# A four-layer network on one core: the group norm's deviation moved to ScalarE, its small products paused, and one step of layer 0 reordered

## The chip, the cores and the metric

The kernel runs as one program on one core of a Trainium2 chip. The metric is the device time of one execution in microseconds (us), the median over several runs. The core has five instruction queues: TensorE (PE: matrix products and transposes), VectorE (DVE), ScalarE (ACT), GpSimd (POOL) and SyncE (SP, which here issues the DMAs). Each queue runs its instructions in its own order, and semaphores join them.

## The reference, cut to what matters

The input `x` is 16 images of 192 channels and 32 × 32 positions, float32. Four residual layers follow one another, each on the group norm of what came before:

```python
# GN: 32 groups of 6 channels, eps 1e-5, no learned scale or shift
def group_norm(x):                       # x: (16, 192, 32, 32)
    g = x.reshape(16, 32, -1)
    g = (g - g.mean(-1, keepdims=True)) / sqrt(g.var(-1, keepdims=True) + 1e-5)
    return g.reshape(x.shape)

x = x + layer0(group_norm(x))   # mLSTM block (12 heads of 32) + SiLU(linear) branch, 3x3 conv, batch norm, leaky relu
x = x + layer1(group_norm(x))   # Mamba block: state-space scan with 16 states
x = x + layer2(group_norm(x))   # depthwise conv, batch norm, relu6
x = x + layer3(group_norm(x))   # scan in 4 directions (SS2D) + local conv branch, mixed by a softmax router
```

This is a sketch of the structure in short names; the batch norms of layers 0 and 2 use statistics over all 16 images, so each of them ends a stage of the program. A group norm is wanted once per image and layer: 64 times.

## The kernel before, in words

Channels lie on partitions (192 as 2 × 96), positions along the free axis. The mean of a group of 6 channels crosses partitions, so `group_norm` works in four stages. DVE takes each channel's mean and variance (`bn_stats`, L351, and `bn_aggr`, L352). A 96 × 96 product on PE with a constant matrix gives the groups' means (L355, 2 columns). DVE forms each channel's deviation from it and its square plus the variance (L357 to L362). A second such product gives the groups' variances (L365). DVE then adds eps (L367) and POOL raises to the power -0.5 (L309, in `pow_mhalf`), which gives the tile `gnr`. The caller scales the image on DVE: `layer0_image` (L543), `layer1_front` (L1240), `layer1_tail` (for layer 2, L1351) and `layer3_front` (L1545).

Layer 0 runs over 128 chunks of 128 positions, 8 for an image. Four chunks make a unit of 512 positions. The loop `for g in range(n + 2)` drives `layer0_step`, which yields up to 8 times for a chunk, and after each yield `side.tick(g + j / 8)` may run a piece of the side tasks. The steps are:

1. `down`, the projection of a unit finished two chunks before;
2. four DVE products `p` of scores and decays (L753), the POOL product `vr` (L755), at a unit's first chunk the unit's decays on PE (`layer0_decays`, L686 and L689), and the next chunk's row of exponents by DMA (`layer0_row`, L700, tile `e`);
3. the carried state times the queries (L767), the weighted values `num` (L779), and two POOL sums on `e` (L705 the mask, L706);
4. the new state (L806) and the exponential of `e` on ACT (L711);
5. the next chunk's scores (L722, first part of `layer0_scores`);
6. transposes of its keys `k` (to `kt`, copied by DVE, L728) and of its values (L733; to `v`, copied by ACT, L736), the second part of `layer0_scores`;
7. the former chunk's output transposes (`layer0_output`, L851), their product with a gate on DVE (`ht`, L854) and a sum on POOL (L857);
8. the norm of the heads (`layer0_norm`, L828 to L841, with Ln and Exp on ACT in L839 and L840).

The side tasks have a window each, from a start to an end in chunks, and are run by it: `image` loads an image and normalises it; `front` does a unit's layer norm (L377 and L385 on PE), up projection (L569, its copies on ACT L571 and L573), convolution, SiLU (L596), query and key projections (L607, key copy L613) and gates, and ends with L619 on ACT, L622 on POOL and three L625 on ACT; `spread` writes a finished image to memory and reads it back as `ya` and `yb`; three `conv` tasks apply the 3 × 3 convolution (L520).

The order on PE is set in two ways. The main instructions of a step are tied to one another in program order by `Chain`:

```python
def __call__(self, ins):
    if self.last is not None:
        self.tc.add_manual_dep(ins.ins, self.last, why)   # NoSync: an order, not a wait
    self.last = ins.ins.name
    return ins
```

The side tasks' products are not tied; a scheduler places them, and everything on the other engines, by its own costs. PE's results for side tasks and for most small steps go to PSUM tiles called `mm`, of which two rotate; a third such product waits until the first one's reader is done.

Layers 1 to 3 share a scan (`scan_run`): for each unit of 512 positions and each of 16 states, in three thirds, ACT makes decays `da` (L986, five buffers) and scaled inputs `xbt` (L966), PE transposes them (`xb`, L994 and L997, three buffers), DVE scans (L1010), POOL multiplies by `c` (L1017) and PE transposes back and sums (`y`, L1028). PE's order there is tied by a list of its own, `in_order`. Loads, group norms and projections of the next images are again side tasks.

Of the kernel before, what the change touches and what calls it, by code (L numbers as in the profile page):

```python
# [19 lines left out]
HP = 96  # L20
# [223 lines left out]
class Chain:  # L244
# [5 lines left out]
    def __call__(self, ins):  # L250
        if self.last is not None:
            why = mybir.DependencyInfo(mybir.DependencyClass.NoSync, mybir.DependencyReason.DATA)
            self.tc.add_manual_dep(ins.ins, self.last, why)
        self.last = ins.ins.name
        return ins
# [19 lines left out]
class Program:  # L275
    def __init__(self, tc, ins, out, at):
        self.tc, self.nc, self.ins, self.out = tc, tc.nc, ins, out
        self.at96, self.at128, self.atc, self.atc0 = at
        self.nb = ins["x"].shape[0]

# [63 lines left out]
    def group_norm(self, pool, psum, x):  # L344

        nc = self.nc
        st = pool.tile([HP, 2, 2, 6], F32, name="gnst")
        mv = pool.tile([HP, 2, 2], F32, name="gnmv")
        for m in range(2):
            for i, h in enumerate(halves()):  # L350
                nc.vector.bn_stats(st[:, m, i], x[:, m, h])  # L351
            nc.vector.bn_aggr(mv[:, m], st[:, m].rearrange("p a b -> p (a b)"))  # L352
            yield 1
        ps = psum.tile([128, 512], F32, name="mm")
        nc.tensor.matmul(ps[:HP, :2], self.k("group", HP), mv[:, :, 0], start=True, stop=True)  # L355
        mean = pool.tile([HP, 2], F32, name="gnmean")
        nc.vector.tensor_copy(mean, ps[:HP, :2])  # L357
        d = pool.tile([HP, 2], F32, name="gnd")
        nc.vector.tensor_tensor(d, mv[:, :, 0], mean, SUB)
        q = pool.tile([HP, 2], F32, name="gnq")  # L360
        nc.vector.tensor_tensor(q, d, d, MUL)
        nc.vector.tensor_tensor(q, q, mv[:, :, 1], ADD)  # L362
        yield 1
        ps = psum.tile([128, 512], F32, name="mm")
        nc.tensor.matmul(ps[:HP, :2], self.k("group", HP), q, start=True, stop=True)  # L365
        r = pool.tile([HP, 2], F32, name="gnr")
        nc.vector.tensor_scalar(r, ps[:HP, :2], EPS, None, ADD)  # L367
        self.pow_mhalf(r)
        yield 1
        return mean, r, d  # L370
# [22 lines left out]
    def layer0(self):  # L393
        tc = self.tc
        with (
# [13 lines left out]
            self.main = Chain(tc)  # L409
            for b in range(1, self.nb):  # L410
                side.add("image", self.layer0_image(b, sp, bp, psum), 8 * b - 5.1, 8 * b - 4)
            for i in range(1, self.nb * S // U):
                side.add("front", self.layer0_front(i, sp, bp, dp, psum), NCH * i - 3.9, NCH * i - 1.2)
            for b in range(self.nb - 1):
                side.add("spread", self.layer0_spread(b, wp, dp), 8 * b + 9, 8 * b + 9.1)
                for j in range(3):
                    at = 8 * b + 9.6 + 2.4 * j
                    side.add("conv", self.layer0_conv2(b, j, bp, psum), at, at + 2.4)
# [11 lines left out]
            side.close()  # L430
            finish(self.layer0_spread(self.nb - 1, wp, dp))
# [307 lines left out]
    def layer0_step(self, g, n, chunks, sp, bp, psum):  # L739
# [52 lines left out]
        if new:  # L792
            yield from self.layer0_scores(new, bp, psum)
        if g - 1 in chunks:
            self.layer0_output(chunks[g - 1], bp, psum)
            yield
        if k:
# [143 lines left out]
    def scan_run(self, units, side, bp, psum):  # L941
# [7 lines left out]
        last = []  # L949

        def in_order(ins):

            if last:
                self.tc.add_manual_dep(
                    ins.ins, last.pop(), mybir.DependencyInfo(mybir.DependencyClass.NoSync, mybir.DependencyReason.DATA)
                )
            last.append(ins.ins.name)
# [97 lines left out]
        for i in range(len(steps) - 2, len(steps)):  # L1055
            for t in range(3):
                total(i, t)
        side.close()
# [11 lines left out]
    def layer12(self):  # L1070
        tc = self.tc
        with (
# [7 lines left out]
            self.rep = 18 * (W + 2), 6  # L1080
            self.stats = wp.tile([HP, 2, 2 * self.nb, 6], F32, name="stats")
# [295 lines left out]
    def layer3(self):  # L1377
        tc = self.tc
        with (
# [7 lines left out]
            self.rep = 19 * (W + 3), 4  # L1387
            self.image = {}
# [322 lines left out]
```

## Time and profile before

| what | us |
|---|---|
| median of 3 runs | 17,355.21 (17,339.39 to 17,372.06) |
| the profiled execution | 17,403.5, its span 17,401.7 |
| PE busy | 15,749.6 (91% of the span) |
| DVE busy | 13,122.0 (75%) |
| ACT busy | 11,873.6 (68%) |
| POOL busy | 11,450.8 (66%) |
| layer 0 | about 0 to 3,860 |
| layers 1 and 2 | about 3,860 to 7,620 |
| layer 3 | about 7,622 to 17,402 |

The profile is of one execution. An engine's busy time says how near it is to being the limit over the whole span; the stages differ, so the waits have to be read in the stage that holds them. In a group of instructions the numbers are the count, the busy time, the mean of one and the idle time ahead of them with what ended it. `PEclk` is the clock that TensorE was granted, in tenths.

### The profile page before, as it was taken

Reading aid. Unit: us, or ns where it says so; the run is one execution under the profiler, and the core shown is the slowest. Engines: PE = TensorE matmul, PEld = TensorE weight load, DVE = VectorE, ACT = ScalarE, POOL = GpSimd, SP = SyncE. Lnnn points to the kernel's source line nnn. Section 1 sums busy time; section 2 is a strip of 40 time slices with the busy share of each in tenths; the row PEclk is TensorE's granted clock in tenths of the full one; section 3 lists DMA queues with packets and bytes.
Section 4 is the critical chain, followed back from the end, with each engine's and each line's share of the span. In section 5 each row is a group of like instructions: output and inputs, shape, how many; then the busy total and the mean of one; then the engine's idle time right before and its main releaser. Section 6 shows DMA issues by size and latency. Waiting matters only on the chain. (4 is left out here: it accounts for less than half of the span.)

```text
span 17401.7 us, 263068 instructions
## 1 busy us (share of the span) xinstructions
PE 15749.6 (91%) x99452; PEld 11013.2 (63%) x99452; DVE 13122.0 (75%) x14859; ACT 11873.6 (68%) x19637; POOL 11450.8 (66%) x5555
## 2 busy tenths in 40 slices
PE   8998988888988899979899999999999999999998
PEld 4444444435555555547777777777777777777777
DVE  4444444437777777749889888888888888888888
ACT  3222322327666666648888888888888888888888
POOL 3333333425555555538788788888878888888888
PEclk8889998989999999989999999999999999999999
DMA  1111111123333343433333333323333333333332
GB/s 51 42 40 44 44 43 44 47 63 107 114 110 110 113 118 116 118 99 103 90 99 107 93 96 101 107 83 99 107 98 92 99 108 88 96 105 102 88 98 67
DMA packets 890141, 1544.65 MB, mean 89 GB/s; under 512 B 83472, under 2 KB 314653, under 8 KB 879530
## 3 DMA queue, kind: packets, MB, share of 16 engines
q1 hardware_dynamic: 888874, 1527.81, 30.3%
q8 instruction: 788, 12.91, 0.3%
q14 instruction: 479, 3.92, 0.1%
HBM read 1284.22 MB, written 243.27 MB: 88 GB/s over the span
## 5 line engine op out<-in xcount | busy, mean ns | idle before, releaser
L1017 POOL TENSOR_TENSOR h<-h,cb 128x1536 f32<-128x1536 f32 x2560 | 8872.8, 3469 | 1432.0 <-DVE h L1010 902.9
L986 ACT ACTIVATE da<-dt,neg_a 128x512 f32<-128x512 f32 x7680 | 5267.0, 714 | 1752.0 <-DVE h L1010 1687.3
L1010 DVE TENSOR_TENSOR_SCAN h<-da,carry,xb 128x512 f32<-128x512 f32 x3840 | 4652.4, 1262 | 657.1 <-PE xb L997 596.2
L1028 PE MATMUL y<-const,h 128*128 128x128 f32 x30720 | 4717.9, 276 | 128.3 <-DVE ysum L1468 54.0
L1010 DVE TENSOR_TENSOR_SCAN h<-da,xb 128x512 f32<-128x512 f32 x3840 | 4440.6, 1202 | 388.7 <-PE xb L997 270.7
L994 PE MATMUL xb<-const,xbt 128*128 128x128 f32 x23040 | 4074.6, 282 | 422.5 <-DVE h L1010 269.3
L966 ACT ACTIVATE xbt<-ut,bt 128x384 f32<-128x384 f32 x7680 | 4174.4, 603 | 246.4 <-PE xb L994 244.3
L994 PEld LDWEIGHTS xb<-const,xbt 128*128 128x128 f32 x23040 | 2757.2, 143 | 1815.5 <-issue 643.8
L1028 PEld LDWEIGHTS y<-const,h 128*128 128x128 f32 x30720 | 3684.9, 143 | 322.8 <-issue 265.4
L997 PE MATMUL xb<-diag,ut 128*128 128x128 f32 x15360 | 3016.4, 279 | 0.0
L997 PEld LDWEIGHTS xb<-diag,ut 128*128 128x128 f32 x15360 | 2383.5, 195 | 63.1 <-issue 63.1
L830 POOL TENSOR_TENSOR hs<-h,mhm 128x384 f32<-128x384 f32 x128 | 108.5, 848 | 1685.1 <-DVE den L835 1290.5
L1016 POOL COPY carry<-h 128x3 f32<-128x3 f32 x1280 | 250.5, 196 | 1220.1 <-DVE h L1010 964.7
L976 POOL TENSOR_TENSOR diag<-const,bt 128x512 f32<-128x512 f32 x640 | 680.8, 1064 | 550.5 <-PE xb L997 362.1
L705 POOL TENSOR_TENSOR e<-e,const 128x1536 f32<-128x1536 f32 x128 | 439.9, 3437 | 288.9 <-DMA e<-row 273.0
L520 PE MATMUL conv<-ya,w_conv 128*64 128x512 f32 (+1 forms) x1152 | 543.9, 656 | 66.1 <-DMA ya<-yrows 62.2
L916 PE MATMUL mm<-dbl,w_dt 45*128 45x512 f32 x960 | 532.8, 639 | 33.6 <-DVE v L1490 16.2
L711 ACT ACTIVATE e<-e 128x1536 f32<-128x1536 f32 x128 | 189.7, 1482 | 417.7 <-POOL e L706 417.4
L854 DVE TENSOR_TENSOR ht<-sz,mm 128x384 f32<-128x384 f32 x128 | 70.7, 552 | 519.5 <-PE mm L851 519.5
L1171 PE MATMUL mm<-rep,t_dw 96*32 96x512 f32 x2304 | 433.5, 614 | 23.5 <-DMA rep<-xr 17.3
L779 PEld LDWEIGHTS num<-v,p 128*128 128x128 f32 x3072 | 389.3, 201 | 102.2 <-issue 77.9
L920 DVE SCALAR_TENSOR_TENSOR dt<-lnsq,mm 128x512 f32<-128x512 f32 x480 | 322.0, 671 | 171.9 <-ACT lnsq L919 171.9
(272 smaller groups left out, 17910.1 us busy)
## 6 DMA issues: line engine op xcount, KB each, us to landing
cb<-row SPq DMA_DIRECT2D x2560, 256.0 KB
rep<-xr SPq DMA_DIRECT2D x384, 331.0 KB
e<-row SPq DMA_DIRECT2D x128, 768.0 KB
rep<-xin SPq DMA_DIRECT2D x384, 256.0 KB
rep<-xr SPq DMA_DIRECT2D x384, 228.8 KB
x<-x SPq DMA_DIRECT2D x48, 768.0 KB
xr<-xin SPq DMA_DIRECT2D x48, 612.5 KB
xr<-xpad SPq DMA_DIRECT2D x32, 867.0 KB
```

The lines of the kernel that those rows point to most:

```text
L520: nc.tensor.matmul(o, self.w_c2[:k, t, c0 : c0 + o.shape[0]], src[:k, r0 : r0 + 16, dx : dx + W], start=t == 0, stop=t == 14, skip_group_c ...
L705: nc.gpsimd.tensor_tensor(k.e, k.e, self.k0("mask")[:, None, :].to_broadcast([128, NH, 128]), ADD)
L916: nc.tensor.matmul(ps, w_dt[:, t * 128 : (t + 1) * 128], dbl, start=True, stop=True)
L966: nc.scalar.activation(t[:, c], u.ut[:, c], AF.Copy, scale=u.bt[:, c, n : n + 1])
L976: nc.gpsimd.tensor_tensor(d, ident[:, None, :].to_broadcast([128, 4, 128]), u.bt[:, 3, n : n + 4][:, :, None].to_broadcast([128, 4, 128]), ...
L986: nc.scalar.activation(da[i, t], u.dt[:, t], AF.Exp, scale=u.neg_a(t, n))
L994: in_order(nc.tensor.transpose(xb[i, t][:, c * 128 : (c + 1) * 128], xbt[i][:, c, t * 128 : (t + 1) * 128], ident))
L997: in_order(nc.tensor.matmul(xb[i, t][:, 384:], u.ut[:, 3, t * 128 : (t + 1) * 128], u.diag[n // 4][:, n % 4], start=True, stop=True, skip_ ...
L1010: nc.vector.tensor_tensor_scan(hv, dv, xv, 0.0 if first else u.carry_in[:, n, t : t + 1], MUL, ADD)
L1017: nc.gpsimd.tensor_tensor(h[i], h[i], u.c.pop(n)[:, None, :].to_broadcast([128, 3, 512]), MUL)
L1028: in_order(nc.tensor.matmul(u.y[:, j], h[i][:, t, c * 128 : (c + 1) * 128], ident, is_transpose=True, start=n == 0 and j % 4 == 0, stop=n ...
L1171: self.nc.tensor.matmul(ps[32 * g : 32 * g + 32], blocks[:, g * side + r], seen, start=r == 0, stop=r == side - 1, skip_group_check=True,)
```

## The change

In `group_norm`, the generator now yields a pause before each of its two small products, so that the side scheduler resumes it no sooner than a set number of steps later: 0.15 chunks in layer 0, 0.7 scan steps in layers 1 and 2, 1.2 in layer 3. Each product is placed behind the last main instruction on PE (`behind`, which orders without becoming part of the chain). The deviation is made by two ACT instructions, Ln with eps as its bias and Exp with scale -0.5, in place of DVE's sum and POOL's power. One `Chain` now serves all layers, and takes the place of `in_order`'s list.

In layer 0 the image task's window moves from 8b - 5.1 ... 8b - 4 to 8b - 6.2 ... 8b - 4.6. The conv tasks start at 8b + 9.9 + 2.3j in place of 8b + 9.6 + 2.4j, with windows of 2.3 in place of 2.4 chunks. In `layer0_step` the former chunk's output transposes stand between the scores and the transposes of `k` and `v`; before they followed both.

The counts change so: 64 DVE instructions (L367) and 64 POOL instructions (L309) fewer, 128 ACT activations more; PE's instructions are the same in number.

```diff
--- before.py
+++ after.py
@@ -247,10 +247,15 @@
     def __init__(self, tc):
         self.tc, self.last = tc, None
 
-    def __call__(self, ins):
+    def behind(self, ins):
+
         if self.last is not None:
             why = mybir.DependencyInfo(mybir.DependencyClass.NoSync, mybir.DependencyReason.DATA)
             self.tc.add_manual_dep(ins.ins, self.last, why)
+        return ins
+
+    def __call__(self, ins):
+        self.behind(ins)
         self.last = ins.ins.name
         return ins
 
@@ -277,6 +282,7 @@
         self.tc, self.nc, self.ins, self.out = tc, tc.nc, ins, out
         self.at96, self.at128, self.atc, self.atc0 = at
         self.nb = ins["x"].shape[0]
+        self.main = Chain(tc)
 
 
     def v96(self, name, i=0, n=1):
@@ -351,8 +357,11 @@
                 nc.vector.bn_stats(st[:, m, i], x[:, m, h])
             nc.vector.bn_aggr(mv[:, m], st[:, m].rearrange("p a b -> p (a b)"))
             yield 1
+        yield Wait(self.pause)
         ps = psum.tile([128, 512], F32, name="mm")
-        nc.tensor.matmul(ps[:HP, :2], self.k("group", HP), mv[:, :, 0], start=True, stop=True)
+        self.main.behind(
+            nc.tensor.matmul(ps[:HP, :2], self.k("group", HP), mv[:, :, 0], start=True, stop=True)
+        )
         mean = pool.tile([HP, 2], F32, name="gnmean")
         nc.vector.tensor_copy(mean, ps[:HP, :2])
         d = pool.tile([HP, 2], F32, name="gnd")
@@ -361,11 +370,12 @@
         nc.vector.tensor_tensor(q, d, d, MUL)
         nc.vector.tensor_tensor(q, q, mv[:, :, 1], ADD)
         yield 1
+        yield Wait(self.pause)
         ps = psum.tile([128, 512], F32, name="mm")
-        nc.tensor.matmul(ps[:HP, :2], self.k("group", HP), q, start=True, stop=True)
+        self.main.behind(nc.tensor.matmul(ps[:HP, :2], self.k("group", HP), q, start=True, stop=True))
         r = pool.tile([HP, 2], F32, name="gnr")
-        nc.vector.tensor_scalar(r, ps[:HP, :2], EPS, None, ADD)
-        self.pow_mhalf(r)
+        nc.scalar.activation(r, ps[:HP, :2], AF.Ln, bias=self.k("eps", HP))
+        nc.scalar.activation(r, r, AF.Exp, scale=-0.5)
         yield 1
         return mean, r, d
 
@@ -406,16 +416,16 @@
             self.unit, self.image = {}, {}
             n = self.nb * S // 128
             side = Side()
-            self.main = Chain(tc)
+            self.pause = 0.15
             for b in range(1, self.nb):
-                side.add("image", self.layer0_image(b, sp, bp, psum), 8 * b - 5.1, 8 * b - 4)
+                side.add("image", self.layer0_image(b, sp, bp, psum), 8 * b - 6.2, 8 * b - 4.6)
             for i in range(1, self.nb * S // U):
                 side.add("front", self.layer0_front(i, sp, bp, dp, psum), NCH * i - 3.9, NCH * i - 1.2)
             for b in range(self.nb - 1):
                 side.add("spread", self.layer0_spread(b, wp, dp), 8 * b + 9, 8 * b + 9.1)
                 for j in range(3):
-                    at = 8 * b + 9.6 + 2.4 * j
-                    side.add("conv", self.layer0_conv2(b, j, bp, psum), at, at + 2.4)
+                    at = 8 * b + 9.9 + 2.3 * j
+                    side.add("conv", self.layer0_conv2(b, j, bp, psum), at, at + 2.3)
             finish(self.layer0_image(0, sp, bp, psum))
             finish(self.layer0_front(0, sp, bp, dp, psum))
             self.layer0_decays(self.unit[0], sp, psum)
@@ -428,6 +438,7 @@
                 for j, _ in enumerate(self.layer0_step(g, n, chunks, sp, bp, psum)):
                     side.tick(g + j / 8)
             side.close()
+            self.main.last = None
             finish(self.layer0_spread(self.nb - 1, wp, dp))
             for j in range(3):
                 finish(self.layer0_conv2(self.nb - 1, j, bp, psum))
@@ -789,11 +800,14 @@
             if new:
                 self.layer0_decay(new)
             yield
-        if new:
-            yield from self.layer0_scores(new, bp, psum)
+        scores = self.layer0_scores(new, bp, psum) if new else iter(())
+        for _ in scores:
+            yield
+            break
         if g - 1 in chunks:
             self.layer0_output(chunks[g - 1], bp, psum)
             yield
+        yield from scores
         if k:
             self.layer0_norm(k, h, sp, bp)
             yield
@@ -946,15 +960,9 @@
         ident = self.k("ident")
         steps = [(u, n) for u in units for n in range(NS)]
         xbt, xb, da, h = {}, {}, {}, {}
-        last = []
-
-        def in_order(ins):
-
-            if last:
-                self.tc.add_manual_dep(
-                    ins.ins, last.pop(), mybir.DependencyInfo(mybir.DependencyClass.NoSync, mybir.DependencyReason.DATA)
-                )
-            last.append(ins.ins.name)
+
+        in_order = self.main
+        in_order.last = None
 
         def times_b(i):
             if i >= len(steps):
@@ -1055,6 +1063,7 @@
         for i in range(len(steps) - 2, len(steps)):
             for t in range(3):
                 total(i, t)
+        in_order.last = None
         side.close()
 
     def untranspose(self, y, t, psum):
@@ -1078,6 +1087,7 @@
         ):
             self.layer1_weights(wp, dp, psum)
             self.rep = 18 * (W + 2), 6
+            self.pause = 0.7
             self.stats = wp.tile([HP, 2, 2 * self.nb, 6], F32, name="stats")
             self.image = {b: {} for b in range(self.nb)}
             side, units = Side(), []
@@ -1385,6 +1395,7 @@
         ):
             self.layer3_weights(wp, bp, dp)
             self.rep = 19 * (W + 3), 4
+            self.pause = 1.2
             self.image = {}
             side, units = Side(), []
             carry = [wp.tile([128, NS, 3], F32, name=f"carry{i}") for i in range(2)]
```

## The prediction

> **What bounds the kernel now.** I read the page's first two parts, then the stretches of the layers, then PE's waits inside layer 0 and who waited for the tile `gnr`. The page first (busy time and share of the span; then tenths busy in 40 slices, and the granted clock in tenths):
>
> ```profile
> PE 15749.6 (91%) x99452; PEld 11013.2 (63%) x99452; DVE 13122.0 (75%) x14859; ACT 11873.6 (68%) x19637; POOL 11450.8 (66%) x5555
> ...
> PE   8998988888988899979899999999999999999998
> ...
> PEclk8889998989999999989999999999999999999999
> ```
>
> PE is the bound throughout; its clock is low only in the first nine slices, layer 0. The stretches are layer 0, layers 1 and 2, and layer 3 (busy us by engine, then clock, DMA share, GB/s):
>
> ```profile
> 0.00:3620.00 3620.00, 3217.96 (x13679) 1630.35 (x13680) 1725.53 (x3452) 1072.12 (x1594) 1369.68 (x846) 0.88 0.18 44
> 3900.00:7600.00 3700.00, 3297.46 (x19328) 2152.27 (x19328) 2759.32 (x3002) 2489.65 (x3973) 2100.95 (x1023) 0.97 0.38 112
> 7622.00:17400.00 9778.00, 9005.87 (x65536) 7120.08 (x65536) 8543.64 (x8204) 8257.47 (x13985) 7913.15 (x3640) 0.97 0.33 97
> ```
>
> In layer 0 PE idles 402 us of 3,620 while the other engines are under half busy: it waits for results late in a queue, not for a full engine. In layer 3 PE, DVE, ACT and POOL are all above 80%. PE's waits in layer 0 (engine, line, what ended the wait: us in all, times, longest):
>
> ```profile
> PE mm L377 <- DVE x L543: 96.8, 15, 7.6
> PE mm L851 <- ACT v L736: 63.1, 22, 4.9
> PE conv L520 <- DMA ya<-yrows: 51.9, 14, 4.9
> PE mm L851 <- DVE kt L728: 43.1, 27, 3.5
> ...
> PE mm L607 <- ACT v L736: 16.0, 15, 1.3
> PE mm L365 <- ACT v L736: 15.2, 13, 1.6
> ```
>
> The six sum to 286 us, 19 us for each of 15 later images. The first is the group norm's own: the unit's projection L377 stands waiting for the normalised image. The tile `gnr` in the whole kernel, first its operations, then its waits:
>
> ```profile
> L367 DVE TENSOR_SCALAR gnr<-mm x64: 122/145/156, 33.5 to 16416.9; 96x2 f32<-96x2 f32 x64
> L309 POOL TENSOR_TENSOR gnr<-gnr,const x64: 679/690/709, 33.7 to 16417.9; 96x2 f32<-96x2 f32 x64
> L543 DVE TENSOR_SCALAR x<-x,gnmean,gnr x32: 798/1394/4699, 34.4 to 3458.7; 96x1024 f32<-96x1024 f32 x32
> ...
>   DVE x L543: 56.3, 16
>   DVE xpad L1545: 24.5, 16
>   DVE xf L1240: 10.9, 16
> ...
>   DVE xpad L1351: 3.2, 4
> ```
>
> The last four rows are DVE waiting for POOL's power: 94.9 us, 52 times. One more wait matters, ACT's in layer 0:
>
> ```profile
> ACT sz L625 <- POOL xact L622: 191.3, 30, 8.2
> ```
>
> **What the Trainium skill says.** "Perfetto Trace Analysis", in "Tensor Engine Instruction (MATMUL, LD_WEIGHTS)", states that ACT, DVE and GpSimd are strict FIFOs: an instruction that waits holds all behind it. The row for L625 agrees: ACT stands 6.4 us a time in front of it. "TensorE: Matmul & The Clock Gate", Part 1, "What's actually happening": the clock halves after an idle window of about 3.4 us and returns after a busy one. The clock of 0.88 in layer 0 against 0.97 agrees; its dips to 0.50 last about 3.4 us or a multiple, and mostly follow idle stretches near 4 us. "ScalarE: Activation LUTs", "Table sets": exp and ln share one table set. The trace has such a pair (L839 212 ns, L840 205 ns), with 2.1 us of idle in all before 121 L840s, so no load lies between them. "SBUF — State Buffer", "SBUF: two separate sides": DVE and GpSimd lock a shared port against each other. L543's 0.80 to 4.70 us for one shape fits.
>
> **The change, part by part.**
>
> *The deviation by ACT.* Removed: 64 L367 (64 × 0.145 = 9.3 us of DVE) and 64 L309 (64 × 0.69 = 44 us of POOL). Added: 128 ACT instructions, priced as L839 and L840: 64 × 0.417 = 27 us. A lone chain shrinks from 0.145 + 0.69 to 0.42 us; more important is the queue it stands in. In layers 1 to 3 ACT's queue is short `da` exponentials (L986, 0.71 us), so I expect the 10.9 + 3.2 us (layers 1 and 2) and 24.5 us (layer 3) of DVE idle to go, with 48 × 0.145 = 7 us of L367. Both lie on the path only as far as DVE limits PE: in layer 3 it nearly does (DVE 87%, PE 92%). Cost there: 32 ACT instructions, 6.7 us in front of `da`, covered by the five `da` buffers. Bounds from -30 to +7.
>
> *Pause and holding.* The built order puts L355 five to eight scans behind the statistics in layers 1 and 2, before two to five; in layer 3 eight to nine. PE's wait for `gnmv` in layers 1 and 2, 74.7 us in 15, then goes. I price it at nothing: under it DVE runs a burst of about 8.3 us (L1235 and L351) in which no scan frees an `xb` buffer, so PE would wait for the scan next. Of layer 3's 41.6 us, 41.2 is one wait at the layer's start, where nothing runs; it stays. Behind the waiting product on PE is the next `xb` transpose; with inputs long ready the product holds it by its own 0.22 us. Upper bound of loss: the norm ends later and its front waits, about 1 us × 48. **Layers 1 and 2: -15 (±30). Layer 3: 24.5 + 2.3 = -27 (±25).**
>
> *Layer 0, the image window, 1.1 chunks earlier.* The built order now has `x` normalised well ahead of L377: -96.8/15 = -6.5 us an image, and L365's 15.2/15 = -1.0, of which the moved pieces give back some 0.7: -6.8. The cost: on ACT the last front pieces change order. In 14 to 16 images the first L625, which waits for POOL's L622 (3.43 us), now stands ahead of the `v` copy L736; before, behind it. PE's L686 (the new unit's decays) needs the `mm` buffer that this copy frees, and there are two. In the trace L622 ends 5.0 us after L686 starts in such units. So L686 waits 5.0 + 0.71 (L625) + 0.47 (L736) + 0.1 = 6.3 us, and the following step a little more because DVE has two L543 ahead of `p`: +6.5. The half clock that followed the old wait follows the new one. **-0.3 us an image (±3).** Without the L622 term it would be -6.8, with no credit for L377 +6.5.
>
> *Layer 0, output transposes ahead of k and v.* L851 no longer stands behind the copies. But L733, now behind it, needs an `mm` buffer freed by ACT's L571, and that one stands behind the exponential L711. The chain to L711's end is the row's DMA (7.3 us from `p` to the mask), 3.44 (L705), 0.83 (L841), 2.75 (L706), 1.48: it ends where it ended. The 4 us stall moves from L851 to L733: -0.2. L607's wait for `v` goes, with a little idle: -0.8. At the image's last chunk L733 waits for `ht` (L854) behind two `p` products on DVE: +1.05, where L851 waited for `kt`. POOL's L857 now stands before L755, which has slack; SP's order of DMAs, the image's load included, is unchanged in the built program, so its queue costs nothing. **+0.05 an image.**
>
> *Layer 0, conv windows.* The built order puts the first L520 at the same place after L851, so the 51.9 us for the DMA `ya` stay: **0**. How long conv's last third keeps PE lightly loaded decides dips of 2 to 14 us an image that follow no long idle; ±5 us an image either way, the largest unknown.
>
> Layer 0: 15 × (-0.3 + 0.05) = -4, say **-5 (±75)**. The total: -5 - 15 - 27 = **-47 us**. The profiled execution took 17,403.5 us (span 17,401.7), 0.28% above the median of the runs, 17,355.21; it would become 17,356, and the median 17,308, -0.27%. About 0.2%, 35 us, is what a measurement of this kernel can tell from no change, so the forecast lies just outside.
>
> **The rivals.**
>
> *The removed stalls are not replaced.* If all six waits vanish (-286) and PE's clock in the three steps that follow them recovers half its loss (read step by step from the granted clock: 8.2 + 3.5 + 2.6 = 14.3 us an image, 15 × 7 = 105), layer 0 gives about -390, all -432: 16,923. For it: the sum of waits is there. Against: each buffer and queue that releases them has a later claimant, named above, and the DMA is untouched. Half of it would give about 17,140.
>
> *Slower: the `v` copy behind L625.* If L622 ends as in the trace but L377's early input brings PE nothing, because the next piece of the front waits for the same ACT queue, L686's 6.3 × 15 = 95 us stand uncovered, plus two half-clock windows (2 × 3.4 × 0.5 = 3.4 us × 15 = 51), less 42: +104, 17,459. For it: the 6.4 us waits at L625. Against: L377's own wait is PE's largest and has one cause. It decides when L622 ends more than about 1 us after L686 could start and the credit for L377 is under half.
>
> *Nothing to measure.* The DVE waits for `gnr` lie beside PE work, and layer 0 trades evenly: 0 to -35, 17,340.
>
> **How the numbers follow.** The forecast with neighbours to -150 has 0.45; the first rival, whole or in part beyond that, 0.13; nothing to measure 0.20; the slower one, whole or in part, 0.22. Faster takes the first two but for a few hundredths: 0.56. Same: 0.21, slower: 0.23. The range runs from 17,190 (-165: the low ends of all three layers, -80 - 45 - 52 = -177, nearly reached) to 17,440 (the slower rival nearly whole). The cases of one sign alone: 17,190 to 17,320.
>
> **What would show it.** Right: PE's row L377 <- `x` gone; a new row of L686 for the `v` copy, about 15 times and 4 to 6 us each; the `v` wait of L851 replaced by one of L733 of like size; conv's DMA row near 50; DVE's rows for `gnr` near zero behind ACT. Wrong: no L686 row and layer 0 over 100 us shorter (first rival), layer 0 longer with the clock under 0.88 (second), or layers 1 to 3 moving by more than 80 us.

## The result, and the profile after

The changed kernel takes 17,541.4 us (median of four runs, 17,520.7 to 17,567.2) against 17,358.5 for the kernel before in the same comparison: a ratio of 1.0107, with a 95% interval of 1.0089 to 1.0125. It is **slower by about 1.1%, 183 us**. The forecast was 17,308 with a range to 17,440. The profiled execution after took 17,554.2 us, its span 17,552.4, 151 us above the profiled span before.

The page first, the lines that answer to those of before:

```profile
PE 15858.4 (90%) x99452; PEld 11102.5 (63%) x99452; DVE 13199.1 (75%) x14795; ACT 11900.5 (68%) x19766; POOL 11409.3 (65%) x5491
...
PE   8988988889888888879999999999999999999998
...
PEclk8888988989999999989999999999999999999999
```

DVE and POOL have 64 instructions fewer each, ACT 129 more (the 128 and a table load), PE the same number. Yet PE is busy 109 us longer with the same count of products: its mean granted clock was lower, 0.945 against 0.951. The stretches of the three stages (busy us by engine, granted clock, DMA share, GB/s), the second and third moved by the time that the stages before them grew:

```profile
0.00:3620.00 3620.00, 3223.72 (x13620) 1681.07 (x13621) 1789.63 (x3424) 1083.60 (x1624) 1364.49 (x829) 0.88 0.17 44
3920.00:7740.00 3820.00, 3358.06 (x19328) 2172.67 (x19328) 2745.02 (x2962) 2504.42 (x4035) 2066.09 (x992) 0.95 0.36 108
7770.00:17550.00 9780.00, 9029.77 (x65551) 7125.36 (x65545) 8560.35 (x8190) 8257.70 (x14019) 7912.22 (x3624) 0.97 0.31 97
```

Layers 1 and 2 stand out: the stretch holds the same 19,328 products as before and is 120 us longer, at 0.95 in place of 0.97. From the trace's scans I take four marks for every kernel below: the first scan of layer 1 (the end of layer 0 and of the loads), first to last scan of layers 1 and 2, the gap to layer 3, and its first to last scan. "Lost" is the time at reduced clock times the missing share; in these traces the clock is either full or half, so a stretch at half clock loses half its length.

| profiled execution | layer 0 to first scan | layers 1, 2 | layer 3 | lost to the clock in layer 0 | in layers 1, 2 | in layer 3 |
|---|---|---|---|---|---|---|
| before | 3,944 | 3,590 | 9,567 | 481 | 92 | 210 |
| after | 3,966 | 3,719 | 9,567 | 497 | 181 | 217 |

One execution of layer 0 is not sharp: the kernels that share its code before gave 3,898 and 3,903 elsewhere, those that share the code after 3,930 to 3,933. Layers 1 and 2 repeat within 20 us. So 130 us come from layers 1 and 2, some 20 to 50 from layer 0, and layer 3 gained nothing.

The mean granted clock is on record for every execution, so the loss of a whole execution can be had without its trace: its span times one minus the clock (which is given to 0.001, so that a mean of four is good to some 10 us). In the mean it is 952 us after and, from one comparison below to the next, 809 to 832 us before. By this account some 120 to 140 of the 183 us are half clock.

**Layers 1 and 2.** PE's waits from 4,500 to 7,500 us (what ended the wait: us in all, times, longest), before:

```profile
PE mm L355 <- DVE gnmv L352: 62.1, 12, 5.2
PE xb L994 <- DVE h L1010: 44.3, 48, 2.5
```

and after, where the scan is L1018 and the depthwise product of layer 2 L1181:

```profile
PE xb L1002 <- DVE h L1018: 107.3, 48, 7.0
PE mm L1181 <- DMA rep<-xr: 46.1, 13, 4.9
PE xb L1002 <- ACT xbt L974: 30.5, 71, 1.9
PE mm L395 <- ACT lnsq L394: 29.9, 21, 2.8
```

The wait for `gnmv` is gone, and its 62 us have moved one line down to the scan: 62.1 + 44.3 = 106.4 before, 107.3 after. That was forecast. The last three rows have grown, from 0.6, 8.7 and 7.2 us before. They say that the side work arrives late: layer 2 waits for the image that the tail has just written to memory, the layer norm for its own squares. By scan steps of an image (32, mean of 11 images), the group norm and layer norm of the next image, steps 13 to 20, take 80.9 us in place of 75.4; the tail and layer 2, steps 23 to 30, 64.2 in place of 59.4; the rest 95.4 and 94.8. An image takes 240.5 us in place of 229.6.

Waits are not the whole of it. Over the two layers PE's idle time rises from 366 to 437 us and the loss to the clock from 92 to 181; the two overlap in part. The stretch from 4,500 to 7,500 us before and after shows it (the third number from the end is the granted clock):

```profile
4500.00:7500.00 3000.00, 2701.47 (x15982) 1764.56 (x15981) 2279.74 (x2476) 2053.75 (x3274) 1735.17 (x844) 0.98 0.39 114
4500.00:7500.00 3000.00, 2635.23 (x15145) 1688.69 (x15146) 2150.73 (x2337) 1963.24 (x3156) 1599.84 (x763) 0.95 0.38 112
```

**Layer 0.** PE's waits to 3,620 us after:

```profile
PE mm L697 <- ACT v L747: 100.6, 14, 8.2
PE mm L744 <- ACT xin L582: 55.1, 19, 5.4
PE conv L531 <- DMA ya<-yrows: 52.0, 14, 4.5
PE mm L744 <- DVE ht L868: 42.8, 30, 3.8
PE mm L580 <- DVE xn L399: 29.9, 24, 3.3
PE mm L778 <- ACT v L747: 22.1, 6, 4.8
```

The row of L377 for `x` (96.8 us before) is gone and the decays (L697, before L686) wait 7.2 us an image for the copy of `v`. The timeline shows why. ACT in one such image (start, length, instruction, and in brackets the idle time before it with its releaser):

```profile
1348.94 0.72 ACT L636 ACTIVATE sz<-sz,p 128x512 f32<-128x512 f32 x1 [8.45 <-POOL xact L633]
1349.57 0.46 ACT L747 COPY v<-mm 128x384 f32<-128x384 f32 x1
```

and PE at the same time:

```profile
1350.08 0.28 PE L697 MATMUL mm<-const,ug 12*128 12x12 f32 x1 [7.31 <-ACT v L747]
```

ACT waits 8.45 us for POOL's L633 (before L622), and the copy, whose transposes on PE (L744) ended at 1,340.9 us, stands behind it.

The tile `gnr` after, its two ACT operations and then DVE's waits for it:

```profile
L377 ACT ACTIVATE gnr<-mm,const x64: 240/258/260, 33.9 to 16572.0; 96x2 f32<-96x2 f32 x64
L378 ACT ACTIVATE gnr<-gnr x64: 186/192/204, 35.5 to 16572.7; 96x2 f32<-96x2 f32 x64
...
  DVE x L554: 11.8, 15
...
  DVE xpad L1361: 1.6, 3
...
  DVE xpad L1556: 1.2, 1
  DVE xf L1250: 1.2, 1
```

0.45 us for the pair where 0.42 was priced, and 15.8 us of DVE waits where there were 94.9.

### The profile page after: what moved, and what is told of

The parts are those of the page before. It is cut to its first block, busy times and chain, and to the rows that moved or that the text cites. A ratio compares the mean times of both kernels' runs of the same rounds, so it can differ in the third digit from the quotient of the medians.

```text
span 17552.4 us, 262990 instructions
## 1 busy us (share of the span) xinstructions
PE 15858.4 (90%) x99452; PEld 11102.5 (63%) x99452; DVE 13199.1 (75%) x14795; ACT 11900.5 (68%) x19766; POOL 11409.3 (65%) x5491
## 5 line engine op out<-in xcount | busy, mean ns | idle before, releaser
L1018 DVE TENSOR_TENSOR_SCAN h<-da,carry,xb 128x512 f32<-128x512 f32 x3840 | 4652.4, 1262 | 678.9 <-PE xb L1005 610.8
L1018 DVE TENSOR_TENSOR_SCAN h<-da,xb 128x512 f32<-128x512 f32 x3840 | 4436.9, 1202 | 395.1 <-PE xb L1005 278.5
L930 PE MATMUL mm<-dbl,w_dt 45*128 45x512 f32 x960 | 530.0, 637 | 32.6 <-DVE v L1501 15.8
L1181 PE MATMUL mm<-rep,t_dw 96*32 96x512 f32 x2304 | 446.2, 629 | 69.1 <-DMA rep<-xr 63.0
L790 PEld LDWEIGHTS num<-v,p 128*128 128x128 f32 x3072 | 435.5, 221 | 109.3 <-issue 82.4
L580 PE MATMUL mm<-xn,w_up 96*128 96x512 f32 x768 | 429.2, 708 | 42.5 <-DVE xn L399 29.9
```

What stands on the lines that cost most here:

```text
L930: nc.tensor.matmul(ps, w_dt[:, t * 128 : (t + 1) * 128], dbl, start=True, stop=True)
L1018: nc.vector.tensor_tensor_scan(hv, dv, xv, 0.0 if first else u.carry_in[:, n, t : t + 1], MUL, ADD)
L1181: self.nc.tensor.matmul(ps[32 * g : 32 * g + 32], blocks[:, g * side + r], seen, start=r == 0, stop=r == side - 1, skip_group_check=True,)
```

## The experiments

Every figure is the median in its own comparison and its ratio to the kernel before there, whose median lay between 17,333 and 17,378 us from one comparison to the next. Expectations that take differences between comparisons carry some 20 us of that. The marks are of one profiled execution, and of one kernel's executions it can be the fastest (e14, e16) or the slowest (e15), so a difference of 20 or 30 us in one mark shows little. "Clock loss" is the mean over all executions of a run; for the kernel before it is 809 to 832 us, for the kernel after 952.

| run | median us | ratio to before, 95% interval | layer 0 | layers 1, 2 | layer 3 | clock loss |
|---|---|---|---|---|---|---|
| e1: after, no pause in layers 1, 2 | 17,343 | 1.0004 (0.9994 to 1.0013) | 3,930 | 3,524 | 9,570 | 840 |
| e2: before, pause in layers 1, 2 added | 17,497 | 1.0086 (1.0070 to 1.0102) | 3,898 | 3,726 | 9,555 | 914 |
| e3: after, pause in the tail only | 17,450 | 1.0059 (1.0044 to 1.0075) | 3,933 | 3,649 | 9,567 | 899 |
| e4: after, copy of `v` ahead of L625 | 17,474 | 1.0069 (1.0054 to 1.0084) | 3,892 | 3,720 | 9,561 | 895 |
| e5: before, products held in layers 1, 2 | 17,334 | 0.9998 (0.9990 to 1.0007) | 3,903 | 3,572 | 9,557 | 805 |
| e6: before, deviation on ACT | 17,250 | 0.9952 (0.9937 to 0.9967) | 3,880 | 3,529 | 9,538 | 781 |
| e7: before, output transposes moved | 17,414 | 1.0044 (1.0029 to 1.0059) | 3,993 | 3,570 | 9,561 | 918 |
| e8: e1 and e4 together | 17,302 | 0.9978 (0.9970 to 0.9985) | 3,906 | 3,535 | 9,572 | 820 |
| e9: e6 with the early image window | 17,359 | 1.0007 (0.9998 to 1.0016) | 3,960 | 3,534 | 9,548 | 856 |
| e10: after, no pause in layer 3 | 17,493 | 1.0092 (1.0075 to 1.0108) | 3,932 | 3,719 | 9,525 | 910 |
| e11: e6 with the conv windows | 17,240 | 0.9943 (0.9928 to 0.9957) | 3,872 | 3,532 | 9,539 | 767 |
| e12: after, output transposes last | 17,475 | 1.0077 (1.0062 to 1.0092) | 3,880 | 3,725 | 9,561 | 900 |
| e13: e12, no pause in layers 1 to 3, layer 0's kept | 17,227 | 0.9933 (0.9918 to 0.9948) | 3,857 | 3,528 | 9,513 | 749 |
| e14: e9, its wait filled with products | 17,322 | 0.9987 (0.9980 to 0.9993) | 3,899 | 3,540 | 9,554 | 790 |
| e15: e9, products held in layer 0 | 17,352 | 1.0008 (1.0001 to 1.0014) | 3,979 | 3,539 | 9,565 | 854 |
| e16: e9 with the conv windows | 17,192 | 0.9913 (0.9898 to 0.9928) | 3,786 | 3,532 | 9,560 | 709 |
| e17: e9 with layer 0's pause | 17,347 | 1.0000 (0.9989 to 1.0011) | 3,957 | 3,542 | 9,547 | 846 |
| e18: e16, products held in the scans | 17,192 | 0.9898 (0.9881 to 0.9914) | 3,809 | 3,545 | 9,524 | 709 |

### The pause

```diff
-            self.pause = 0.7      # layer12, e1
+            self.pause = 0
```

> The changed kernel with the pause of layers 1 and 2 set from 0.7 to 0 scan steps; the rest of the change stays. Theory A (the pause makes the front and the tail of an image late against their windows, and what follows bunches): an image of layers 1 and 2 falls from 240.5 us to 227 to 231, the first to the last scan of the two layers from 3,719 to 3,560 to 3,600, the whole by about 130 to 150 us to some 17,400. Rival B (the products held behind the main chain, or Ln and Exp in ACT's queue): no more than 30 us of the 130 go. Rival C (a carry-over from layer 0, as the shift of the clock's windows): nothing goes.

The whole loss against the kernel before goes, and layers 1 and 2 fall 195 us, to 65 below before. PE's waits in e1, 4,500 to 7,500 us, begin so:

```profile
PE mm L363 <- DVE gnmv L358: 61.9, 12, 5.2
```

The wait that the pause had removed is back at its old size while the stage is 195 us shorter. It was free, as the prediction held; the pause was not. Of the 195 us some 96 are half clock (the stage's loss in the trace falls from 181 to 85 us), and PE's idle time there falls from 437 to 311 us. Over all executions the loss is 840 us here and 952 in the changed kernel.

```diff
+        yield Wait(self.pause)    # ahead of both products; 0.7 in layers 1, 2, else 0 (e2, on before)
```

> The kernel before with one thing added: a pause of 0.7 scan steps ahead of each of the two small products in layers 1 and 2. No holding, the deviation still by DVE and POOL, layer 0 as before. Theory A: the pause alone is enough; an image goes from 229.6 to about 240 us, the whole from 17,358 to about 17,490 (+110 to +150). Rivals B and C: within 30 us of the kernel before.

The pause alone is enough: +0.86%. PE's waits in e2, same stretch:

```profile
PE mm L357 <- DVE gnmv L353: 62.0, 12, 5.2
PE mm L1175 <- DMA rep<-xr: 60.8, 13, 6.0
PE mm L380 <- DVE xf L1244: 49.6, 12, 4.7
```

Without holding, the pause does not even remove the wait for `gnmv`; it doubles the layer norm's wait for `xf` (24.5 us before) and adds layer 2's for `xr`. The stage's loss to the clock doubles as well, to 189 us. Steps 13 to 20 of an image take 81.3 us, as in the changed kernel, but steps 18 and 19 only 24.4.

```diff
-        mean, r, _ = yield from self.group_norm(sp, psum, x)       # layer1_front, e3
+        mean, r, _ = yield from self.group_norm(sp, psum, x, 0)    # pause 0 for this one
```

> The changed kernel with the pause left out of layer1_front's group norm alone; layer1_tail's keeps its 0.7. Theory A with two places of like size: scan steps 13 to 20 of an image (the front) fall from 80.9 to about 75 us, steps 23 to 30 (the tail and layer 2) stay near 64; the whole falls by about 70 us against the changed kernel. If one place causes both, either nothing or all of the 130 us goes.

Steps 13 to 20 fall to 74.6 us, steps 23 to 30 stay at 64.2: two places, each paying for its own pause. They are not of like size: layers 1 and 2 get 70 us shorter here, and e1 takes off another 125 for the tail. From the last statistics to the first scaling an image's norm takes 8.9 us in the front before, 13.6 after and 6.7 in e1; in the tail 17.8, 20.7 and 16.3.

```diff
-            self.pause = 1.2      # layer3, e10
+            self.pause = 0
```

> The changed kernel with layer 3's pause set from 1.2 to 0; everything else of the change stays, its pause in layers 1 and 2 too. With the deviation on ACT alone layer 3 took 9,538 us from first to last scan, in the changed kernel 9,567. If the pause takes back the gain: 9,535 to 9,548 here and the whole 20 to 30 us below the changed kernel. If the holding does: 9,560 or more.

The pause costs layer 3 some 40 us: 9,525 without it. The six kernels with it (after, e1, e3, e4, e8, e12) took 9,561 to 9,572, the three with held products and no pause there (e10, e13, e18) 9,513 to 9,525. PE's idle time in that layer is the same in both groups, about 650 us; the loss to the clock is 207 to 218 us with the pause and 169 to 186 without.

### The deviation and the holding

```diff
-        nc.vector.tensor_scalar(r, ps[:HP, :2], EPS, None, ADD)      # e6, on before
-        self.pow_mhalf(r)
+        nc.scalar.activation(r, ps[:HP, :2], AF.Ln, bias=self.k("eps", HP))
+        nc.scalar.activation(r, r, AF.Exp, scale=-0.5)
```

> The kernel before with Ln and Exp on ACT in place of DVE's sum and POOL's power, in all layers; no pause, no holding, layer 0's order as before. Theory H: layers 1 and 2 fall by 15 us at most, layer 3 (9,567 us) by 0 to 25 us as the DVE waits for gnr go; the whole -40 to 0. Its rival (ACT brings the 65 us): layers 1 and 2 near 3,530.

-0.48%, the part that brings the gain. In layers 1 and 2 it is worth 40 to 60 us, not 15: the leg from the second product to the scaling falls from 3.6 to 1.4 us in the front and 2.9 to 1.6 in the tail, and PE's idle time in the stage from 366 to 311 us at an equal loss to the clock. (With the pause, in the changed kernel, the front's leg is 3.5 us again.) Layer 3 is 29 us shorter in this execution, as expected, but that is not shown to be the deviation: the seven kernels that share this layer 3 (e6, e9, e11, e14 to e17) took 9,538 to 9,565, in the mean 10 us less than the four with that of before, and PE's idle time in it is no shorter (675 us here, 674 before). In layer 0 L377's wait for `x` falls too, 96.8 to this:

```profile
PE mm L377 <- DVE x L543: 57.2, 16, 4.9
```

```diff
+        self.held.behind(nc.tensor.matmul(...))    # both products, layers 1 and 2 only (e5, on before)
```

> The kernel before with one thing added: in layers 1 and 2 the two small products stand behind the last main instruction of PE. Without the pause the changed kernel's layers 1 and 2 took 3,524 us from first to last scan against 3,590 before; this and the next run ask which part brings the 65 us. Theory H (holding: PE no longer stands on L355 for gnmv, 5.2 us an image): 3,525 to 3,545 and the whole 45 to 65 us shorter, 17,280 or so. The prediction's view (holding is worth nothing, since a scan is waited for next): 3,580 to 3,595, the whole within 20 us.

No difference. The prediction's nought for the holding stands, in layers 1 and 2.

### Layer 0

```diff
+        self.copied(nc.scalar.copy(k.v[...], ...))             # an order on ACT, e4
-            nc.scalar.activation(sz[:, t], ...)
+            self.copied.behind(nc.scalar.activation(sz[:, t], ...))
```

> The changed kernel with one order added in layer 0: the three L625 of a unit (L636 in the changed kernel) stand behind the newest copy of v on ACT. The prediction's mechanism (L686, L697 in the changed kernel, waits for the copy behind L625, which waits for POOL): PE's wait of L697 for v, 100.6 us in 14, falls below 15, layer 0 gets shorter by 60 to 110 us with its half clock, the whole to about 17,450. Rival: the wait passes to the next thing on ACT's queue (the exponential of e, or the group norm's Ln behind L625) and layer 0 changes by less than 30 us.

The row of L697 for `v` goes, and the whole falls by about 0.4%, so the mechanism is real. But the waits do not fall to nothing. PE's first two rows in e4's layer 0, behind conv's DMA row (55.2 us):

```profile
PE mm L376 <- DVE gnq L372: 53.4, 15, 5.7
PE mm L781 <- ACT v L750: 45.4, 11, 5.5
```

```diff
-        if new:
-            yield from self.layer0_scores(new, bp, psum)
+        scores = ...      # as in the change: scores, output transposes, k and v (e7, on before)
```

> The kernel before with layer 0's output transposes between scores and k, v, and nothing else. The changed kernel is about 70 us longer than before outside layers 1 and 2; theory P (the prediction's pricing): this move alone is worth 0 to +20 us, since the stall passes from L851 to L733, and layer 0 stays at 3,898 to 3,944. Theory Q (the move sets the copy of v late on ACT, so that the decays L686 and the state wait): +50 to +90 us, layer 0 above 3,950.

Theory Q's size, +0.44%, though at one only of the two places that it named: L767 waits for the copy of `v` (28.8 us), the decays do not. Chunk by chunk PE's idle time is the same as in e5, whose layer 0 is that of before (2.84 and 2.86 us a chunk). What grew is the clock's loss, 437 to 580 us in layer 0; over all executions it is 918 us against 814 before. The windows from 400 to 3,800 us, e5:

```profile
400.00:3800.00 3400.00, 3045.38 (x13162) 1534.47 (x13160) 1622.20 (x3239) 982.66 (x1478) 1297.81 (x805) 0.90 0.17 43
```

and e7, where PE is busier with fewer products done:

```profile
400.00:3800.00 3400.00, 3083.99 (x12990) 1580.50 (x12990) 1591.42 (x3229) 985.56 (x1475) 1295.64 (x799) 0.86 0.17 43
```

> The changed kernel with layer 0's output transposes back after k and v; all else of the change stays. In the kernel before the move alone cost about 80 us. If that cost is the same within the change: 17,440 to 17,470, layer 0 below 3,900, PE's row of L697 (the decays) for v gone, since the copy of v stands ahead of L625 again. Rival (the early image or the conv windows set the layer's loss): less than 30 us.

This is the opposite edit, on the changed kernel. 0.3% comes back, and the row of L697 is gone. So the move is needed for L625 to stand ahead of the copy, but it takes more than the move: e7, which has it alone, shows no such row (nor does e9, the image window alone).

```diff
-                side.add("image", ..., 8 * b - 5.1, 8 * b - 4)      # e9, on e6
+                side.add("image", ..., 8 * b - 6.2, 8 * b - 4.6)
```

> The kernel before with the deviation on ACT (as in the run of that alone, 17,250 us) and layer 0's image window moved as in the changed kernel; output transposes last, conv windows and all else as before. Theory R (the earlier image is a gain where the copy of v stays ahead of L625): PE's wait of L377 for x, 57 us there, falls below 10, layer 0 by 30 to 60 us to 3,820 to 3,850, the whole to 17,195 to 17,220. Rival (a later claimant takes it): within 15 us of 17,250.

A miss. L377's wait does fall below 10 us, but the whole rises by 0.55%. The norm's Ln now holds the `mm` buffer that the next step needs:

```profile
PE mm L767 <- ACT gnr L367: 47.1, 13, 4.0
```

Again PE's idle time is unchanged (2.35 us a chunk, 2.42 in e6), and the clock's loss is up, 445 to 522 us (781 to 856 over all executions).

```diff
+            if g % 8 == 3 and g > 8:     # e14, on e9: ahead of L767
+                for _ in range(12):
+                    self.main(nc.tensor.matmul(num_flat[:, :128], ident, q, start=True, stop=True))
```

> The run with the early image window (17,359 us, 109 above the deviation on ACT alone) with added work that nothing reads: twelve 128x128 products ahead of L767 in the fourth chunk of each later image, written into num before its own products overwrite it. There PE waits 3.4 us an image for gnr, and with a warm clock the twelve take about as long. Theory K (the idle time is as long as before the shift, and what costs is the half clock that follows it, 7 us an image more): layer 0 falls from 3,960 to 3,860 to 3,910 though PE does more work. Rival (the wait's place is what costs, whatever the clock): layer 0 stays at 3,960 or rises by up to 15 x 3.3 = 50 us.

PE does 12 products more an image, and the median is 37 us lower, by the ratios 0.2%. Over all executions the loss falls from 856 to 790 us while the rest of the time grows by 28. (The profiled execution, in which layer 0 is 61 us shorter and its loss 406 us in place of 522, was the fastest of the 20.) From 400 to 3,800 us, e9 and then e14:

```profile
400.00:3800.00 3400.00, 3119.14 (x13039) 1588.76 (x13038) 1593.59 (x3209) 986.15 (x1500) 1294.09 (x787) 0.88 0.17 43
```

```profile
400.00:3800.00 3400.00, 3099.12 (x13515) 1586.85 (x13516) 1580.86 (x3222) 987.80 (x1504) 1295.66 (x791) 0.91 0.17 44
```

So the early window's cost, some 95 us, is mostly half clock: 75 us of loss came with it, and filling the wait takes 66 away. The Trainium skill's "TensorE: Matmul & The Clock Gate", Part 1, "What's actually happening", says that an idle window of about 3.4 us halves the clock and a busy one restores it; that filling a wait of 3.6 us an image takes away 66 us of loss agrees. For the output move the same reading rests on the granted clock alone; its waits were not filled.

> The deviation on ACT alone (17,250 us) with the conv tasks' windows of the changed kernel. The prediction's view: the first L520 stays where it is, its wait for ya stays near 52 us, the whole within 20 us of 17,250. Rival: other dips of the clock in the first chunk of an image (8 to 10 us an image lost there), 30 to 75 us either way.

The conv windows alone (9.9 + 2.3j) do next to nothing, as forecast.

> The early image window with the two small products of all layers held behind the main chain (its reach in layer 0; in layers 1 to 3 no main instruction is tied there). With window, holding, pause and conv windows together layer 0 took 3,880 us, with the window alone 3,960. If the holding is what makes the early window harmless: 3,870 to 3,910. If the pause of 0.15 or the conv windows do: 3,940 to 3,970.

> The early image window with the pause of 0.15 chunks in layer 0 alone. The complement of the run with the conv windows: if the pause makes the window harmless, layer 0 at 3,870 to 3,910 and the whole at 17,250 to 17,290; otherwise 3,940 to 3,980.

> The early image window (17,359 us, layer 0 at 3,960) with the conv tasks' windows of the changed kernel as well. Holding did not make the window harmless; if the conv windows do, because they place other products behind the wait: layer 0 at 3,870 to 3,910, the whole at 17,250 to 17,290. If the pause of 0.15 does: 3,940 to 3,980 and 17,340 to 17,370.

With the early image, neither holding nor pause helps, and the conv windows turn a loss into a gain: 17,192 us, where e9 has 17,359. e9's row of L767 for `gnr` is gone. Layer 0's loss falls to 346 us and it is 94 us shorter than e6's; over all executions the loss is 709 us against 781 in e6, which is about the whole difference. The first rows of PE's waits in e16's layer 0:

```profile
PE conv L520 <- DMA ya<-yrows: 50.9, 15, 4.7
PE mm L851 <- ACT v L736: 41.3, 19, 6.3
PE mm L733 <- DVE xn L389: 32.9, 28, 3.6
PE mm L806 <- POOL xin L561: 31.8, 12, 4.3
```

### The sums

> The changed kernel with both repairs: no pause in layers 1 and 2, and L625 behind the newest copy of v. If the two add: 17,541 - 198 - 67 = 17,276, some 65 us below the kernel before. If they share a cause: 17,310 to 17,345.

Short of the sum: 0.22% below before, not 0.4%.

> The changed kernel with three of its parts undone: no pause in layers 1 and 2, none in layer 3, output transposes last. Deviation on ACT, holding, and layer 0's windows stay. If the three costs add (198, 48 and 67 us): 17,541 - 313 = 17,228. If they overlap or the holding costs something by itself: 17,250 to 17,300.

17,227: the three costs add, as nearly as the spread can tell.

> The best run so far (deviation on ACT, early image, conv windows, 17,192 us, layer 0 at 3,786, layer 3 at 9,560) with the products held behind the main chain in the scans of layers 1 to 3 alone, not in layer 0; no pause anywhere. The run with holding everywhere and layer 0's pause had layer 3 at 9,513 but layer 0 at 3,857. If holding helps layer 3 and holding or the pause hurts layer 0: 3,780 to 3,800 and 9,510 to 9,530, the whole at 17,140 to 17,170. If layer 3's difference is only the spread between executions: 17,180 to 17,205.

Layer 3 is 36 us shorter than in e16, layers 1 and 2 and layer 0 longer by 13 and 23; the median is the same (the kernel before was 28 us slower in e18's comparison, 17,378 to 17,349). The marks speak for holding in layer 3 (9,513 to 9,525 in the three kernels with it and no pause, 9,538 to 9,565 in the seven with neither), the medians do not tell; it stays open.

e18 and e13 differ in nothing but layer 0's pause and holding, which e13 has: 0.9898 against 0.9933, 0.35% or 60 us, with intervals that do not meet. PE's wait for the second small product's input, e18 and then e13:

```profile
PE mm L375 <- DVE gnq L371: 2.6, 2, 1.8
PE mm L375 <- DVE gnq L371: 35.9, 13, 5.1
```

Which of the two costs was not separated: beside the early image without the conv windows (e15, e17) neither made a difference. e16 and e18 are the best kernels here: the deviation on ACT and both windows of layer 0, no pause, output transposes last, 0.9% to 1.0% below the kernel before.

## Why the prediction was wrong, point by point

**The step that failed** is "Upper bound of loss: the norm ends later and its front waits, about 1 us × 48", and with it "Layers 1 and 2: -15 (±30)". Measured +130 us in the trace, and without the pause -65: the pause costs 195 us there, 6 to 7 us for each of the 30 norms that run beside the scans (e1, e2, e3), and some 40 us in layer 3 (e10). The norm ends not 1 us later but 4.7 in the front and 2.9 in the tail, and 6.9 and 4.4 later than in e1. Nor has the bound a term for the clock, which is about half of the cost in layers 1 and 2. I had read the page's clock row as low "only in the first nine slices", but layers 1 to 3 of the kernel before lose about 300 us to it too.

I had read the pause as a delay of one product. It delays the rest of a task whose window stays where it was: `Side` hands out pieces by the share of the window that has passed, so what falls due meanwhile is handed out at once when the pause ends (steps 18 and 19 of an image take 36.1 us in place of 25.0), and the task's reader, layer 2's load of `xr`, begins just after the image is written. That the pause is the cause is shown. That this bunching is how the front pays is not: e2 pays as much there with steps 18 and 19 no longer than before.

**Right:** PE's wait for `gnmv` was worth nothing; the scan was waited for next, by the same 62 us. Holding is nought in layers 1 and 2. The deviation on ACT: its price, and DVE's waits for `gnr`. For layers 1 and 2 its -15 was too small; it left out that everything after the norm starts earlier. **Not shown:** layer 3's -27. One execution has -29 (e6), the mean of seven kernels about -10, and no idle time of PE went, which was the ground given for it.

**Layer 0** was priced at -5 (±75) and is up some 20 to 50 us, inside the range, but by parts that were not priced so. The waits came as forecast: L377's row gone, L686 behind the copy of `v` behind L625 (6.3 us forecast, 7.2 measured), L851's wait passing to L733 (55.1 us), conv's DMA row unchanged at 52.0. That L686's row came was partly luck: the prediction laid it to the image window, and it goes when the output move goes (e12). In sum PE's idle time did trade evenly (about 2.9 us a chunk before and after). The term that was mis-sized is the half clock, which I let "follow" the wait at an equal price. It does not: the output move alone costs 0.44% at equal idle time (e7). The clock's dips do not "mostly follow idle stretches near 4 us" either: of 82 dips in layer 0 of the kernel before (from 100 us on), 42 begin in, or within 4 us after, a stretch of 3 us or more without a product, and 34 have none over 2 us there. That my ±5 us an image had no sign was the error; whole parts have one. By the medians the two windows together gain 0.39% (e16 against e6), layer 0's pause and holding, which have no term of their own in the prediction, cost 0.35% (e13 against e18), and the output move 0.30% (e12): +0.26%, 45 us. The early image's cost (e9) is not among them, since the conv windows stand beside it in the change.

**The rivals.** The slower one named L625's queue. It is a part (e4), but not the largest. The largest, the pause, was in none of them, so the range ended too low. The prediction's own sign of error, layers 1 to 3 moving by more than 80 us, is what showed it.

## What to carry to other kernels

A pause in a task that has a due time is a delay of everything after it: leave it out, or move its window and its reader's with it (which no run here tried). Do not price a moved wait by its length alone: the same idle time lost more to the clock in one place than in another. Read the granted clock of each stage, and of every execution, beside the waits. Try the parts of a bundle singly and in pairs: here one part paid, two cost, and one that did nothing alone was worth 0.9% beside another.

## What the runs showed of the hardware that I had not expected

- Work that nothing reads made the kernel faster: twelve 128x128 products in a wait of 3.6 us an image took 66 us of half-clock loss away (mean of all executions) and 37 us off the median.
- Most of what the parts of this change cost was half clock, in stages whose mean clock looks high: in layers 1 and 2 it is 0.95 in place of 0.97, and 89 us.
- Two ACT instructions of 0.26 and 0.19 us in place of one of 0.15 us on DVE and one of 0.69 us on POOL shortened the leg to the scaling by 2.2 us in the front. The instructions themselves became 0.4 us shorter; the rest was waiting in queues and between engines.
